# Two products of the keys on VectorE, denominators on TensorE, and two lists for the last part of an attention layer

## The chip, the cores and the metric

The kernel runs on one core of one Trainium2 chip. A core has five engines that run side by side, each through its own queue in order: TensorE (PE: matmuls and transposes), VectorE (DVE), ScalarE (ACT), GpSimd (POOL) and SyncE (SP, which issues most DMAs). Matrix products land in PSUM, everything else lies in SBUF. The metric is device time of one execution in microseconds; less is better. Comparisons use the median of several runs. One further execution was recorded by the profiler; all rows of the profile belong to that one.

## What is computed

Four graph layers follow each other on a graph of N = 2708 nodes with 128 features. Each is `x = x + layer(relu(layernorm(x)), adj)`. The change lies in layer 1, an attention with one head of 8 numbers for each of 128 channels d:

```python
q = (x @ Wq.T).reshape(d, n, h)        # d = 128, n = 2708, h = 8; k and v likewise
a = jnp.einsum('dnh,dmh->dnm', q, k) * scale
a = a + spatial_encoding + edge_encoding   # both are adj
a = jax.nn.softmax(a, axis=2)
out = jnp.einsum('dnm,dmh->dnh', a, v).reshape(n, h * d)
return out @ Wo.T
```

`adj` is nearly all zeros (some five entries a row). The kernel uses this. For all pairs of nodes without an edge the exponential of q·k is a polynomial of third degree in q and k, so the sums over m can be taken once as moments of the keys and evaluated for each query. For the pairs with an edge the kernel adds what the edge changes: exp(q·k) (exp(2 adj) - 1), times v for the numerator and alone for the denominator.

## The kernel before

**The pairs of channels.** The main loop of layer 1 runs over D = 64 pairs d of channels. Each pass has six chunks c. A chunk turns features of the queries (`turn`: transposes f_ps on PE, a copy fT on ACT), evaluates them against the weighted moments (`evaluate`: matmuls g_ps on PE, L1538; then on DVE the product z, L1546, and a reduction o_raw, L1555), and prepares what later passes need: the queries' features fq of pair d+1 (products on DVE through `mul_v`, L802), the moments m_ps of pair d+1 (PE, L869), and the keys' features fk of pair d+2 (products on POOL through `mul_g`, L805). `features` holds the products under names: "p0" to "p2", "xy" (16 products for each node, 704 numbers per partition), "t0" (10 products, 440 numbers), "t1", "t2". Which chunk makes which is written out in the tables `turns_q` and `turns_k`: "xy" in chunk 2, "t0" in chunk 3. For queries one operand is a copy in PSUM (kq_ps); for keys both are in SBUF (kv_t). `with_values` makes y, the keys' values times their first features (POOL, 704 numbers, twice a pass).

**The slots.** Between the chunks a generator `first` is advanced: 1.75 steps a chunk at the start, 4 from `faster` on, when `from_neighbours` begins. This walks over 121 slots b: a tile t of 128 nodes (sorted by number of neighbours) and one neighbour of each. A slot takes six steps: `load` fetches keys and values of the neighbours (indirect DMA, POOL's queue, L1235) for slot b+2, and `values` multiplies the values of slot b-2 by their weights (DVE, L1274); `store`, and `logits` of slot b (a product of 1024 numbers on POOL, L1250); `summed` reduces it for slot b-1 into c_c in PSUM (DVE, L1256); `added` adds slot b-2 to the tile's sum by a matmul with the identity (PE, L1291, v_ps); `weigh` (slot b-1: ACT, exponential and weight in place in c_c; in a tile's first slot also a copy c_den); `copied_out` at a tile's end. The denominators are added in `values` by DVE (c_den, L1282), in all slots of a tile but the first.

**The last part.** When the slots are over, each chunk takes up to four `step`s of other work: `normalise(u)` loads the two parts of a unit's sums (SP), adds them (POOL, L1395), takes reciprocals (DVE, L1400), multiplies (DVE, L1405) and stores the result in o_d (SP, L551); `projected(t)` loads 128 nodes from o_d (SP, L1034), transposes (PE, L1043), multiplies by Wo (PE, L1061) and adds to x (DVE, L1065). A unit is two groups of four channels, but for the last two units, which are one group each. All stand in one list, `beside`, taken strictly in order; a head of the list that cannot start holds up the rest. A generator yields how many chunks it wants to wait (LOAD is 4). What is left after the last pass is worked off in a loop of its own, and then layer 2 begins (L1846).

All instructions stand in the queues in the order of this code; the framework adds the waits.

Of the kernel before, what the change touches and what calls it, by code (L numbers as in the profile page):

```python
# [46 lines left out]
def gnn4_kernel(  # L47
# [687 lines left out]

    def features(mul, k, k2, f, most):

        T = k.shape[1]
        n = k.shape[0]
        gs = k[:, :, :HEAD].rearrange("p t (g e) -> p t g e", g=2)  # L740
        hs = k2[:, :, :HEAD].rearrange("p t (g e) -> p t g e", g=2)
        two = f[:, :, XX : XX + 20].rearrange("p t (g w) -> p t g w", g=2)
        yy = f[:, :, YY : YY + 10]

        def pair(e, o):
            w = 3 - e
            mul(
                two[..., o : o + w],
                gs[..., e : e + 1].to_broadcast([n, T, 2, w]),
                hs[..., e + 1 : 4],  # L750
            )

        def triple(o, left, right):
            w, v = left.shape[2], right.shape[2]
            if v == 1:
                mul(f[:, :, o : o + w], left, right.to_broadcast([n, T, w]))
            else:
                mul(
                    f[:, :, o : o + w * v].rearrange("p t (a b) -> p t a b", a=v),
                    left[:, :, None].to_broadcast([n, T, v, w]),  # L760
                    right[:, :, :, None].to_broadcast([n, T, v, w]),
                )
# [8 lines left out]
        return {  # L771
            "sq": lambda: nc.scalar.activation(two[..., 3:7], gs, AF.Square),  # L772
            "lin": lambda: nc.scalar.copy(f[:, :, LIN : LIN + 4], k[:, :, 4:8]),
            "p0": lambda: pair(0, 0),
            "p1": lambda: pair(1, 7),
            "p2": lambda: pair(2, 9),
            "xy": lambda: triple(XY, k2[:, :, 0:4], k[:, :, 4:8]),
            "t0": lambda: triple(YYY, yy, k[:, :, 4:5]),
            "t1": lambda: triple(YYY + 10, yy[:, :, 4:], k[:, :, 5:6]),
            "t2": lambda: triple(YYY + 16, yy[:, :, 5:7], k[:, :, 6:8]),  # L780
            "n": norms_of,
        }
# [32 lines left out]

    copied, turned_ = {}, {}

    def of_pair(d, at):
# [11 lines left out]
    def keys(d):  # L830
# [4 lines left out]
        fks[d] = fkp[d % 2]  # L835
        return features(mul_g, kv, kv, flat(fks[d]), most2[:, 1, 2 * d : 2 * d + 2])

# [232 lines left out]

    LOAD, SOON = 4, 1

    with ExitStack() as ph:
# [135 lines left out]
        def from_neighbours():  # L1211
# [46 lines left out]
            def weigh(b):  # L1258
# [5 lines left out]
                nc.scalar.activation(c, c, AF.Copy, scale=cw[:sz, t, s0 : s0 + 1])  # L1264
                if s0 == 0:
                    dens[t] = sm.tile([P, C], FP, name="c_den")
                    nc.scalar.copy(dens[t][:sz], c)

            def values(b):
# [10 lines left out]
                )  # L1280
                if s0:
                    nc.vector.tensor_tensor(dens[t][:sz], dens[t][:sz], c, ALU.add)  # L1282

            def added(b):
# [5 lines left out]
                for j in range(2):  # L1290
# [72 lines left out]
        def unit_of(g):  # L1363
            return g // 2 if g < NG - 2 else g - NG // 2 + 1

        NU = unit_of(NG - 1) + 1

        def normalise(u):

            last, two = u == NU - 1, u < NU - 2  # L1370
            nh = GRP * (1 + two)
            h0 = nh * u if two else (NG - NU + u) * GRP
            g = h0 // GRP
# [49 lines left out]
        beside = []  # L1423
        done = 0
        late, final = [], []
        for t, (r0, sz) in enumerate(rows):
            need = unit_of(min((((r0 + sz) * P - 1) // N) // GRP, NG - 1))
            while done <= need:
                beside.append((done, done, True))
                done += 1  # L1430
                while late and late[0][1] <= done - 2:
                    beside.append(late.pop(0))
            if need < NU - 1:
                late.append((t, need, False))
            else:
                final.append(t)
        beside += late
        groups = [(t, min(t + 4, final[0])) for t in range(0, final[0], 4)]
# [22 lines left out]
        def sum_bank():  # L1461
            return ps_c.tile([P, 2, S, C], FP, name="c_c")[:, 0, 0]

# [5 lines left out]

        def begin(summed):  # L1470

            if not beside:
                return None
            i, need, norm = beside[0]
            last = norm and i == NU - 1
            if need >= summed and not last:
                return None
            if not norm and any(e[2] <= need for e in under_way):
                return None
            takes = 1 if norm and i >= NU - 2 else 2  # L1480
            for ring in ("big",) if norm else ("c_v", "c_q"):
                if sum(e[4] for e in rings[ring]) + takes <= room[ring]:
                    beside.pop(0)
                    gen = normalise(i) if norm else projected(i, ring)
                    entry = [gen, None, need if norm else NU, True, takes]
                    rings[ring].append(entry)
                    under_way.append(entry)
                    return entry
            return None

        def step(n, summed):
# [3 lines left out]
            if entry is None:  # L1495
                entry = begin(summed)
# [117 lines left out]
        with tc.manual_schedule():  # L1614
# [7 lines left out]
            for d in range(D):  # L1622
                asked, keyed = {}, {}
                for c in range(NCH):
# [60 lines left out]
            for e in under_way:  # L1685
                e[1] = min(e[1], n)
            while beside or under_way:
                if to_turn:
# [498 lines left out]
```

## Time and profile before

| What | us |
|---|---|
| median of 3 runs (2151.46 to 2160.33) | 2151.55 |
| the profiled execution, its time | 2157.09 |
| its span (first to last instruction) | 2155.3 |
| PE busy, share of the span | 1692.6 (79%) |
| DVE busy | 1444.2 (67%) |
| ACT busy | 931.8 (43%) |
| POOL busy | 1321.0 (61%) |
| first reduction of a slot (L1256) starts | 754.2 |
| last one starts | 1464.4 |
| last z of the pairs (L1546) starts | 1714.9 |
| layer 2's first matmul (L1846) starts | 1765.2 |

A row of the profile names a line of the kernel, the engine and operation, output<-inputs with their sizes (partitions x elements), how often it ran, its busy time in us and the mean of one in ns, and how long the engine was idle just before and for whom. Busy shares are averages over stages with different limits: what matters is which engine is full in the stage that a change touches. Durations of matmuls are modelled by the profiler and overlap each other.

### The profile page before, as it was taken

How to read it: one execution, taken by the hardware profiler on the slowest of the kernel's cores; microseconds unless marked ns; L12 is line 12 of the kernel's file. 1: busy time of each engine (PE TensorE's matmuls, PEld its weight loads, DVE VectorE, ACT ScalarE, POOL GpSimd, SP SyncE). 2: the span in 40 equal slices, each digit the busy share in tenths (PEclk: the TensorE clock that was granted, in tenths of full speed). 3: DMA queues.
4: the chain of work that ended last, by engine and by line, in shares of the span. 5: the costliest groups of instructions: out<-in, count | busy, mean ns of one | idle time of the engine just before them, and what ended most of it. 6: DMA issues, size and time to landing. Idle time of an engine off the chain costs nothing. (4 is left out here: it accounts for less than half of the span.)

```text
span 2155.3 us, 30079 instructions
## 1 busy us (share of the span) xinstructions
PE 1692.6 (79%) x10634; PEld 1348.4 (63%) x10634; DVE 1444.2 (67%) x3232; ACT 931.8 (43%) x2049; POOL 1321.0 (61%) x1363
## 2 busy tenths in 40 slices
PE   4767989988889788988888888888889769943442
PEld 3656864488789666666666665667889745423431
DVE  6899846366677788888888888877788720134331
ACT  3947744376677444444444444444445210021010
POOL 1343332066566699999999999997667210057762
PEclk9978999999999999999999999988999979965555
DMA  4755319778799676667766766764767757433331
GB/s 158 298 164 191 134 57 363 294 246 249 240 300 318 177 245 239 225 238 255 252 231 240 237 244 245 250 237 143 228 202 223 242 152 276 155 138 104 94 100 38
DMA packets 256854, 453.68 MB, mean 210 GB/s; under 512 B 112267, under 2 KB 180110, under 8 KB 231483
## 3 DMA queue, kind: packets, MB, share of 16 engines
q1 hardware_dynamic: 225459, 282.79, 39.6%
q0 software_dynamic: 31232, 168.86, 23.0%
q8 instruction: 85, 1.39, 0.3%
q14 instruction: 78, 0.64, 0.1%
HBM read 336.99 MB, written 114.60 MB: 210 GB/s over the span
## 5 line engine op out<-in xcount | busy, mean ns | idle before, releaser
L1538 PE MATMUL g_ps<-mw,fT 128*124 128x124 f32 x2816 | 377.9, 277 | 10.8 <-DVE mw L883 6.2
L869 PE MATMUL m_ps<-y,fk 123*128 123x128 f32 (+1 forms) x2816 | 372.6, 278 | 0.2 <-POOL fk L805 0.2
L1538 PEld LDWEIGHTS g_ps<-mw,fT 128*124 128x124 f32 x2816 | 344.5, 192 | 12.0 <-DVE mw L883 7.1
L869 PEld LDWEIGHTS m_ps<-y,fk 123*128 123x128 f32 (+1 forms) x2816 | 345.6, 194 | 1.3 <-issue 1.0
L1528 ACT COPY fT<-f_ps 128x496 f32<-128x496 f32 (+1 forms) x384 | 208.6, 543 | 242.1 <-PE f_ps L1524 239.9
L1291 PE MATMUL v_ps<-c_v,ident 128*128 128x512 f32 (+1 forms) x484 | 254.3, 651 | 74.7 <-DVE c_v L1274 74.0
L805 POOL TENSOR_TENSOR fk<-kv_t 128x264 f32<-128x264 f32 (+3 forms) x256 | 188.5, 761 | 186.4 <-ACT kv_t L833 185.6
L1546 DVE TENSOR_TENSOR z<-g_ps,bq 124x360 f32<-124x360 f32 (+1 forms) x384 | 191.1, 498 | 163.3 <-PE g_ps L1538 151.0
L1524 PE MATMUL f_ps<-ident,fq 124*128 124x124 f32 x1408 | 222.9, 278 | 94.1 <-DVE fq L802 63.8
L1250 POOL TENSOR_TENSOR c_kv<-c_kv,c_q 128x1024 f32<-128x1024 f32 (+1 forms) x121 | 284.3, 2350 | 5.0 <-DMA c_kv<-kv_n,srt 3.4
L1524 PEld LDWEIGHTS f_ps<-ident,fq 124*128 124x128 f32 x1408 | 167.4, 145 | 188.5 <-issue 90.1
L805 POOL TENSOR_TENSOR y<-kv_t 128x704 f32<-128x704 f32 x128 | 191.0, 1492 | 67.6 <-PE m_ps L869 67.0
L1555 DVE TENSOR_REDUCE o_raw<-z 124x72 f32<-124x360 f32 (+1 forms) x384 | 190.7, 497 | 13.2
L1291 PEld LDWEIGHTS v_ps<-c_v,ident 128*128 128x128 f32 (+1 forms) x484 | 86.8, 200 | 151.7 <-DVE c_v L1274 69.2
L1256 DVE TENSOR_REDUCE c_c<-c_kv 128x128 f32<-128x1024 f32 (+1 forms) x121 | 148.0, 1223 | 50.2 <-POOL c_kv L1250 47.7
L1263 ACT ACTIVATE c_c<-c_c 128x128 f32<-128x128 f32 (+1 forms) x121 | 31.7, 262 | 330.6 <-DVE c_c L1256 312.9
L805 POOL TENSOR_TENSOR fk<-fk,kv_t 128x440 f32<-128x440 f32 (+2 forms) x192 | 154.9, 821 | 5.5 <-ACT fk L772 5.3
L1274 DVE TENSOR_TENSOR c_v<-c_kv,c_c 128x1024 f32<-128x1024 f32 (+1 forms) x121 | 146.6, 1211 | 0.0
L1235 POOL DMA_INDIRECT c_kv<-kv_n,srt x121 | 118.0, 975 | 22.3 <-issue 8.6
L1974 POOL DMA_INDIRECT g<-tab_d,l_nbr x99 | 103.5, 1045 | 30.2 <-issue 29.8
L957 PE MATMUL qkv_ps<-wT,hT 128*128 128x512 f32 (+1 forms) x264 | 116.9, 601 | 0.4 <-ACT hT L438 0.4
L170 POOL TENSOR_TENSOR n_hot<-n_hot,n_fl 128x640 f32<-128x640 f32 (+1 forms) x22 | 34.0, 1545 | 119.6 <-DVE n_hot L164 116.0
(315 smaller groups left out, 2989.0 us busy)
## 6 DMA issues: line engine op xcount, KB each, us to landing
a_nat<-in_adj_dram SPq DMA_DIRECT2D x34, 1354.0 KB
raw<-qkv_d SPq DMA_DIRECT2D x128, 275.0 KB
qkv_d<-qkv SPq DMA_DIRECT2D x21, 1600.0 KB
n_raw<-qkv_d SPq DMA_DIRECT2D x96, 275.0 KB
kv_n<-n_kv SPq DMA_DIRECT2D x16, 1408.0 KB
fk<-in_adj_dram SPq DMA_DIRECT2D x12, 1354.0 KB
o_g<-o_raw SPq DMA_DIRECT2D x31, 396.0 KB
fq<-in_adj_dram SPq DMA_DIRECT2D x9, 1354.0 KB
```

The source lines that it names most:

```text
L805: nc.gpsimd.tensor_tensor(o, x, y, ALU.mult)
L869: nc.tensor.matmul(pms[d][:, :P], fks[d][:sz, t].rearrange("p i f -> p (i f)"), wide[h][:sz, o : o + P], start=t == 0, stop=t == NT - 1,)
L1235: nc.gpsimd.indirect_dma_start(out=kvs[b][:sz, e].rearrange("p c e k -> p (c e k)"), out_offset=None, in_=kv_n.rearrange("n c k -> n (c k) ...
L1250: nc.gpsimd.tensor_tensor(k, k, qs[t][:sz], ALU.mult)
L1256: nc.vector.reduce_sum(cs[b][:sz], kvs[b][:sz, 0, :, 0], axis=AX.X)
L1274: nc.vector.tensor_tensor(z[:sz], kv[:sz, 0, :, 1].rearrange("p (j c) k -> p j c k", j=2), c.rearrange("p (j c) -> p j c", j=2)[:, :, :, None]
L1291: nc.tensor.matmul(accs[t][:sz, j], ident[:sz, :sz], z[:sz, j].rearrange("p c k -> p (c k)"), start=s0 == 0, stop=s0 == ROOM[t] - 1,)
L1524: nc.tensor.transpose(pt[:, m, :USED], fqs[d][:USED, t0 + m].rearrange("p i f -> p (i f)"), ident[:USED, :USED])
L1528: nc.scalar.copy(fts[d, c][:, :n, :USED], pt[:, :n, :USED])
L1538: nc.tensor.matmul(pg[:USED, m, :USED], ft[:, m, :USED], mws[d][:, :USED], start=True, stop=True,)
L1546: nc.vector.tensor_tensor(z[:USED, : 2 * n], pg[:USED, :n] .rearrange("p m (i w) -> p (m i) w", i=2)[:, :, : VW * B_ALL] .rearrange("p a ( ...
L1555: nc.vector.reduce_sum(ros[g][:USED, t0 : t0 + n, i : i + 2].rearrange("p m i k -> p m (i k)"), z[:USED, : 2 * n].rearrange("p (m i) k b - ...
```

## The change

During the slots (from `faster` to the end of `first`, while the list `crowded` holds something) the keys' products "xy" and "t0" are made by `mul_v` on DVE instead of `mul_g` on POOL. The denominators of the slots are no longer added on DVE: `weigh` copies the weights of every slot to c_den (ACT), and `added` adds that copy by one more matmul with the identity, into a third or fourth quarter of the PSUM tile c_c, which grows from [P, 2, S, C] to [P, 4, S, C] (S = 1, C = 128). `copied_out` reads it there.

In the last part the list `beside` becomes two, `to_norm` and `to_project`. A new unit is tried first; a projection starts when all units that it reads are `settled`, LAND = 4 chunks after their stores were issued. The last six groups are units of their own. LOAD becomes 5, and `normalise` ends with its store.

```diff
-    def features(mul, k, k2, f, most):
+    def features(mul, k, k2, f, most, heavy=None):
...
-        def triple(o, left, right):
+        def triple(o, left, right, mul=mul):
...
-            "xy": lambda: triple(XY, k2[:, :, 0:4], k[:, :, 4:8]),
-            "t0": lambda: triple(YYY, yy, k[:, :, 4:5]),
+            "xy": lambda: triple(XY, k2[:, :, 0:4], k[:, :, 4:8], heavy or mul),
+            "t0": lambda: triple(YYY, yy, k[:, :, 4:5], heavy or mul),
...
-        return features(mul_g, kv, kv, flat(fks[d]), most2[:, 1, 2 * d : 2 * d + 2])
+        return features(
+            mul_g, kv, kv, flat(fks[d]), most2[:, 1, 2 * d : 2 * d + 2],
+            mul_v if crowded else None,
+        )
...
-    LOAD, SOON = 4, 1
+    LOAD, SOON, LAND = 5, 1, 4
...
-            c_two = ps_c.tile([P, 2, S, C], FP, name="c_c")
+            c_two = ps_c.tile([P, 4, S, C], FP, name="c_c")
...
-                if s0 == 0:
-                    dens[t] = sm.tile([P, C], FP, name="c_den")
-                    nc.scalar.copy(dens[t][:sz], c)
+                dens[b] = sm.tile([P, C], FP, name="c_den", bufs=3)
+                nc.scalar.copy(dens[b][:sz], c)
...
-                if s0:
-                    nc.vector.tensor_tensor(dens[t][:sz], dens[t][:sz], c, ALU.add)
...
+                nc.tensor.matmul(
+                    c_two[:sz, 2 + t % 2, 0],
+                    ident[:sz, :sz],
+                    dens.pop(b)[:sz],
+                    start=s0 == 0,
+                    stop=s0 == ROOM[t] - 1,
+                )
...
-                    nc.scalar.copy(acc[:sz, :, HEAD], dens.pop(t)[:sz])
+                    nc.scalar.copy(acc[:sz, :, HEAD], c_two[:sz, 2 + t % 2, 0])
...
-            return g // 2 if g < NG - 2 else g - NG // 2 + 1
-
-        NU = unit_of(NG - 1) + 1
+            return g // 2 if g < 2 * TWOS else g - TWOS
+
+        TWOS = NG // 2 - 3
+        NU = NG - TWOS
...
             store_heads(nc.sync, h0, on)
-            yield SOON
...
+            crowded.append(True)
...
+        def begin(n, summed):
+
+            entry = None
+            if to_norm and (to_norm[0] < summed or to_norm[0] == NU - 1):
+                u = to_norm[0]
+                entry = enter("big", 1 + (u < TWOS), normalise(u), u)
+                if entry is not None:
+                    to_norm.pop(0)
+            if entry is None and to_project:
+                t, need = to_project[0]
+                if all(settled.get(u, n + 1) <= n for u in range(need + 1)):
+                    for ring in ("c_v", "c_q"):
+                        if entry is None:
+                            entry = enter(ring, 2, projected(t, ring), None)
+                    if entry is not None:
+                        to_project.pop(0)
+            return entry
...
+                if entry[2] is not None:
+                    settled[entry[2]] = n + LAND
...
+                            crowded.clear()
```

More of the change, by code (lines that the diff above doesn't have):

```diff
@@ L816, in gnn4_kernel @@
     copied, turned_ = {}, {}
+    crowded = []
     def of_pair(d, at):
@@ L1363, in unit_of @@
         def unit_of(g):
-            return g // 2 if g < NG - 2 else g - NG // 2 + 1
-        NU = unit_of(NG - 1) + 1
+            return g // 2 if g < 2 * TWOS else g - TWOS
+        TWOS = NG // 2 - 3
+        NU = NG - TWOS
         def normalise(u):
-            last, two = u == NU - 1, u < NU - 2
+            last, two = u == NU - 1, u < TWOS
             nh = GRP * (1 + two)
-            h0 = nh * u if two else (NG - NU + u) * GRP
+            h0 = nh * u if two else (TWOS + u) * GRP
             g = h0 // GRP
@@ L1419, in faster @@
             pace[0] = 4.0
+            crowded.append(True)
             yield
         first = chain(by_node(), sorted_rows(), faster(), from_neighbours())
-        beside = []
-        done = 0
-        late, final = [], []
+        to_norm, to_project = list(range(NU)), []
+        final = []
         for t, (r0, sz) in enumerate(rows):
             need = unit_of(min((((r0 + sz) * P - 1) // N) // GRP, NG - 1))
[L1428 to L1432, printed above, removed]
             if need < NU - 1:
-                late.append((t, need, False))
+                to_project.append((t, need))
             else:
                 final.append(t)
-        beside += late
+        settled = {}
         groups = [(t, min(t + 4, final[0])) for t in range(0, final[0], 4)]
@@ L1461, in sum_bank @@
         def sum_bank():
-            return ps_c.tile([P, 2, S, C], FP, name="c_c")[:, 0, 0]
+            return ps_c.tile([P, 4, S, C], FP, name="c_c")[:, 0, 0]
         def projected(t, ring):
@@ L1468, in projected, with enter @@
             yield from project_out(both, turn_bank, sum_bank, woT, t)
-        def begin(summed):
-            if not beside:
-                return None
[L1474 to L1489, printed above, removed]
+        def enter(ring, takes, gen, unit):
+            if sum(e[4] for e in rings[ring]) + takes > room[ring]:
+                return None
+            entry = [gen, None, unit, True, takes]
+            rings[ring].append(entry)
+            under_way.append(entry)
+            return entry
[14 more added lines that the diff above has]
+                        to_project.pop(0)
+            return entry
         def step(n, summed):
@@ L1495, in step @@
             if entry is None:
-                entry = begin(summed)
+                entry = begin(n, summed)
             if entry is None:
@@ L1686, in gnn4_kernel @@
                 e[1] = min(e[1], n)
-            while beside or under_way:
+            while to_norm or to_project or under_way:
                 if to_turn:
```

## The prediction

> **What bounds the kernel now.** I read the page's engine rows over 40 slices first, then the busy time of each engine in the stretches between landmarks, then waits and timelines inside them. The chain that ended last names only the final 3 us and is of no use here.
>
> ```profile
> DVE  6899846366677788888888888877788720134331
> POOL 1343332066566699999999999997667210057762
> 759.00:1469.40 710.40, 611.44 (x3782) 457.76 (x3782) 596.84 (x1090) 309.86 (x813) 677.71 (x552) 0.97 0.68 239
> 1469.40:1716.00 246.60, 214.35 (x1780) 206.23 (x1780) 196.97 (x432) 109.00 (x252) 148.69 (x114) 0.94 0.71 207
> 1716.00:1760.00 44.00, 23.71 (x112) 20.17 (x112) 13.07 (x32) 9.52 (x21) 7.26 (x3) 0.67 0.65 187
> ```
>
> The last three rows give, after the length, PE, weight load, DVE, ACT, POOL, clock, DMA share and GB/s. In the stretch of the slots POOL is busy 677.7 of 710.4 us (95%): it is the bound. The stretch holds 60 rows of L883, two for each pair of channels d, so it is 30 pairs of 23.68 us; per pair POOL has 22.59 us of work, PE 20.38, DVE 19.89, ACT 10.33. Afterwards PE is nearest its limit (214 of 247 us), and from 1716 to 1760 nothing is: a drain of loads, normalisation and out-projection that follow each other. The change touches all three.
>
> **Products moved to DVE.** Per form, in the slots:
>
> ```profile
> L805 POOL TENSOR_TENSOR fk<-kv_t 128x704 f32<-128x704 f32 x30 | 44.1, 1469 | 0.6
> L805 POOL TENSOR_TENSOR fk<-fk,kv_t 128x440 f32<-128x440 f32 x30 | 31.7, 1058 | 0.0
> L1282 DVE TENSOR_TENSOR c_den<-c_den,c_c 128x128 f32<-128x128 f32 x98 | 27.4, 280 | 0.0
> L802 DVE TENSOR_TENSOR fq<-bq,kq_ps 128x704 f32<-128x704 f32 x30 | 26.4, 878 | 0.0
> ```
>
> "xy" and "t0" take 1.47 + 1.06 = 2.53 us per pair from POOL: 22.59 becomes 20.06. DVE gets them at 0.88 us (the query's product of the same shape, fourth row) and 0.61 us (mean of the query's 440-element form), and loses the additions to c_den, 27.4/30 = 0.91 us. So DVE becomes 19.89 + 0.88 + 0.61 - 0.91 = 20.47 us. "t0" reads what POOL wrote a chunk earlier and "n" reads none of it, so no new wait on data arises.
>
> But the query's products have one operand in PSUM (kq_ps); the key's have both in SBUF (kv_t). The only DVE product in this trace with two SBUF operands beside a busy POOL is L1405:
>
> ```profile
> 1495.14 2.17 DVE L1405 TENSOR_TENSOR r_c<-r_o,r_rs 128x704 f32<-128x704 f32 x2
> 1495.19 4.23 POOL L805 TENSOR_TENSOR fk<-kv_t 128x264 f32<-128x264 f32 x4
> 1498.51 3.33 DVE L1405 TENSOR_TENSOR r_c<-r_o,r_rs 128x704 f32<-128x704 f32 x2
> 1499.38 1.70 POOL L805 TENSOR_TENSOR fk<-fk,kv_t 128x440 f32<-128x440 f32 x1
> ```
>
> Undisturbed it takes 0.88 us (its minimum), on average 1.34, at most 3.19; POOL's own 440-element product took 1.70 instead of 1.06 us beside it. The Trainium skill, "SBUF — State Buffer", section "SBUF: two separate sides", has the rule that speaks against the change: a DVE instruction with two SBUF inputs and a GpSimd instruction exclude each other for their whole length. By rows of busy time alone POOL gains 2.53 us per pair; by the rule it gives back the products' 1.49 and gains 1.04. The rows side with the rule. DVE's own wait for a POOL product under way: from 0 to 2.35 us each (POOL's longest product); at L1405's mean excess (1.34 - 0.88 = 0.46) two would be 0.9 us per pair. I take 0.4, because part falls where DVE waits anyway.
>
> **Denominators on TensorE.** One 128x128 matmul per slot, two passes. Nearest row: m_ps<-y,fk, 8 passes in 1.06 us of which 0.28 is one pass's own length, so 0.12 us per pass: 4 x 0.24 = 0.95 us per pair, PE 21.3 us. ACT's 99 further copies cost 0.265 us each (the 22 existing ones), 0.9 us per pair, hidden: ACT is busy 44%.
>
> What is not hidden is where the sum lies. c_two grows to [P, 4, 1, 128] floats, 2 KB a partition, and holds both the logits' sums (written by DVE, rewritten by ACT, read by DVE) and now the matmul's target. The Trainium skill, "PSUM — Partial Sum Buffer", section "PSUM bank collisions raise a hardware error", says that two engines may not touch one 2 KB bank at once, different columns and reads included, so that software has to order them. That this program is so ordered shows in before:
>
> ```profile
>   DVE tab L1951: 8.7, 7
> ACT fq L773 <- DVE fq L802: 10.7, 17, 0.7
> ```
>
> The first stands in the answer on the PSUM tile ab_ps, under who waited for its users: DVE did, 8.7 us, seven times of seven, although L1951 reads other columns of it than ACT's L1950. In the second ACT's copy from kq_ps waits for DVE's product from it, without using its result. So the dens matmul of slot b-2 will wait for DVE's reduction of slot b-1 emitted before it, and everything behind it on PE with it: transposes f_ps and products g_ps, for which DVE's next z waits. By columns alone this wait would be nothing; by bank it is what the order of the queues makes it. The phase of slots against chunks is fixed (6 steps against 4): in chunks 0 and 3 the reduction is a chunk ahead of its matmul, in chunks 2 and 5 directly ahead. Chunk 2:
>
> ```profile
> 1001.97 1.98 PE L1291 MATMUL v_ps<-c_v,ident 128*128 128x512 f32 x4 [0.31 <-DVE c_v L1274]
> 1002.84 0.88 DVE L802 TENSOR_TENSOR fq<-bq,kq_ps 128x704 f32<-128x704 f32 x1
> 1003.64 1.22 DVE L1256 TENSOR_REDUCE c_c<-c_kv 128x128 f32<-128x1024 f32 x1
> 1003.79 0.59 PE L1524 MATMUL f_ps<-ident,fq 124*128 124x124 f32 x4
> 1005.28 0.53 DVE L1546 TENSOR_TENSOR z<-g_ps,bq 124x360 f32<-124x360 f32 x1 [0.42 <-PE g_ps L1538]
> ```
>
> PE runs ahead: f_ps starts at 1003.79 while DVE reduces until 1004.86, and z then waits only 0.42 us. Afterwards f_ps must follow the matmul, which follows the reduction; the key's "xy" stands just ahead of that reduction too. From the reduction's end to z: hand-over 0.06, matmul 0.24, then f_ps to z as above, 1005.28 - 1003.79 = 1.49: 1.8 us in which DVE is idle. In chunk 5 likewise. Two per pair make 3.6 us, against 0.42 + 0.77 at the same places of the pair at 1000 us.
>
> **Sum of a pair.** Before, DVE: 19.89 busy + 1.96 waiting for g_ps (58.8 us in all idle before z) + 1.4 for POOL's logits (42.3 us) + small ones = 23.68. After: 20.47 busy + 3.6 at the two places + 0.5 left of the other waits before z (0.77 before) + 0.4 for the port + 0 for POOL (2.5 us lighter) = 24.97. That is +1.29 us, over 30 pairs +39 us. PE's own account agrees: 21.3 work + about 2 stalled + 1.5 still waiting for c_v = 24.8. So the bound moves from POOL to the loop DVE-PE-DVE, and POOL's gain is idle time. Bounds: -1.0 us (no bank wait) to +1.7 (port wait at 0.9), -30 to +51 us.
>
> **The last part.** Six last groups become units of their own (two before), normalisation goes ahead of projection, and a projection's load is issued four chunks after the store that it needs. From 1480 to 1716 SP stood some 47 us for PE at L1034 and 89 for DVE at L551, but hardly anybody in the loop waited for that: PE's wait for o_nat is 0.6 us there. What can shrink is the drain:
>
> ```profile
> 1711.38 11.57 SPq L1034 DMA_DIRECT2D o_nat<-o_d  x1
> 1725.29 3.54 POOL L1395 TENSOR_TENSOR r_o<-r_o,r_c 128x1584 f32<-128x1584 f32 x1 [21.93 <-DMA r_c<-more_n]
> 1744.31 1.86 POOL L1395 TENSOR_TENSOR r_both<-o_raw,r_both 128x792 f32<-128x792 f32 x1 [12.50 <-DMA r_both<-more_n]
> ```
>
> A double unit is still added at 1725, ten us after the last z, and the last unit at 1744 only, because its load stood behind o_nat loads. Four projections (transposes from 1720 on) lie in the drain. Afterwards, from the last z at 1716: addition of the unit of group 30 1.9, reciprocal and product 1.6, store and load of o_nat about 7 (as from the store at 1733.4 to the transposes at 1741.9, less what stood between), transposes and copies 3, sums 3.7, addition and statistics 0.9, normalising and turning the last group about 6 (1753 to 1760): 24 us instead of 44. Against -20: three projections move into the PE-bound loop at 1.04 + 1.95 = 3.0 us, +9. The finer units cost four more of each: five issues on SP at 0.3 to 0.6 us, which stand beside waits; a reciprocal pair 2 x 0.68 instead of 1.25, nothing. Together -11 us, bounds -25 and +8 (PE pays, drain stays).
>
> **Forecast.** The profiled execution has a span of 2155.3 and a time of 2157.09 us; the median of the three runs is 2151.55, 5.5 less, and I count from it: 2151.55 + 39 - 11 = 2179.5; a profiled execution would show about 2185.
>
> **Rivals.**
> 1. *POOL was the bound and is relieved* (faster). If PE's wait at the bank is absent or covered, a pair is POOL's 20.06 + 1.09 gaps + 1.49 lost to the port = 22.6, -32 us; with -11: 2108. It decides once the two stalls cost DVE under 0.3 us each beyond today's. For it: POOL's 95%. Against it: the seven waits of ab_ps. 12%.
> 2. *The stall is half covered*: PE has slack of 3 us per pair and DVE can run values ahead; a pair then stays near 23.9, +7, with -11: 2148, no difference that can be told. 16%.
> 3. *The last part pays too*: slots at the upper bound +51, last part +8: 2211. For it: PE at 87% there. 12%.
>
> The forecast itself, 2160 to 2200 as its own range, gets 60%. A measurement of this kernel tells about 0.5% (10.8 us) from no change. Rival 1 and a sliver of 2 are faster: 0.14; most of 2 and the forecast's lowest edge no change: 0.15; the rest slower: 0.71. The range 2142 to 2206 leaves out rival 1 and most of 3.
>
> **What would show it.** Right: POOL in the slots falls to about 85%; PE's matmul into c_c waits for DVE's L1256 some 2 us per pair; idle time before z rises from 59 to over 100 us; the stretch of the slots grows to about 750 us; the key's products on DVE show means above 0.88 and 0.61 with maxima over 2 us; the drain from last z to L2's first matmul shrinks by some 20 us. Wrong: POOL still over 92% with a shorter stretch (rival 1), or a longer stretch with no wait of PE at c_c, which would leave the port alone to blame.

## The result, and the profile after

The changed kernel takes 2302.13 us (median of 4 runs, 2298.21 to 2308.45) against 2154.41 us for the kernel before in the same comparison: a ratio of 1.0685, 95% interval 1.0648 to 1.0721. It is slower, as forecast, but by 148 us, where 28 were forecast and 2206 us was the upper end of the range.

The profiled execution of the changed kernel took 2298.21 us (span 2296.4), 141.1 us more than that of before. The table splits this at the same landmarks in both traces: first row of L883 (L887 after) in the slots, the same row behind the last slot, last z, layer 2's first matmul.

| stage | before | after | change | forecast |
|---|---|---|---|---|
| slots, 30 pairs | 710.4 | 830.6 | +120.2 | +39 |
| loop, to the last z | 245.5 | 268.3 | +22.8 | +9 |
| drain, to layer 2 | 50.3 | 51.1 | +0.8 | -20 |
| the rest | 1149.1 | 1146.4 | -2.7 | 0 |

The engine rows over 40 slices of the changed kernel's page:

```profile
DVE  6899754566778777777777777776878840042332
POOL 1334222266656777767777677774666500027774
```

In the slots (slices 14 to 28) POOL's row shows sixes and sevens where it stood at nines before. Neither row has a nine there, and by the busy times below no other engine is near its limit, so no engine is the bound by its work alone. These are the busy times in the three stages (stretch, length, then PE, weight load, DVE, ACT and POOL busy, clock, DMA share, GB/s):

```profile
758.86:1589.42 830.56, 668.99 (x4021) 508.44 (x4020) 646.12 (x1052) 329.75 (x912) 614.18 (x492) 0.95 0.58 204
1589.42:1857.70 268.28, 212.31 (x1690) 204.31 (x1690) 204.37 (x425) 104.33 (x241) 155.81 (x116) 0.87 0.72 203
1857.70:1908.80 51.10, 29.83 (x206) 25.65 (x206) 14.03 (x43) 15.53 (x34) 2.15 (x7) 0.84 0.31 107
```

In the slots POOL is at 614 of 831 us (74%), PE at 81%, DVE at 78%. DVE stands idle for 184 us of it. For whom, the list of waits in the slots says (who waited <- for whom: us in all, times, longest):

```profile
ACT c_c L1267 <- PE c_c L1299: 441.9, 119, 8.9
DVE z L1556 <- PE g_ps L1548: 137.5, 60, 3.4
PE c_c L1299 <- DVE c_c L1260: 83.5, 51, 5.5
...
DVE c_v L1277 <- ACT n_kv L1320: 18.4, 17, 1.7
...
DVE c_v L1277 <- ACT c_den L1270: 12.7, 26, 0.5
```

Before, the wait of z in the slots was:

```profile
DVE z L1546 <- PE g_ps L1538: 51.2, 46, 3.3
```

L1299 is the new matmul for the denominators. PSUM holds more than matrix products here: DVE writes the logits' sums into c_c, and ACT works on them there. The matmul waits 83.5 us for DVE's reduction L1260, which writes other columns of the same PSUM bank and whose result it does not read; ACT's exponential of those logits in turn is released by the matmul. DVE's z, two stations behind it on PE, waits 137.5 us instead of 51.2. The last two rows of the first list are new altogether: DVE's values now wait for ACT's copies out of the same bank.

One chunk of the timeline shows the chain (start, length, engine, line, and in brackets the idle time before it):

```profile
1018.72 1.98 PE L1292 MATMUL v_ps<-c_v,ident 128*128 128x512 f32 x4 [0.53 <-DVE c_v L1277]
...
1019.40 0.88 DVE L802 TENSOR_TENSOR fq<-bq,kq_ps 128x704 f32<-128x704 f32 x1
...
1020.20 0.89 DVE L802 TENSOR_TENSOR fk<-kv_t 128x704 f32<-128x704 f32 x1
...
1021.00 1.22 DVE L1260 TENSOR_REDUCE c_c<-c_kv 128x128 f32<-128x1024 f32 x1
...
1022.36 0.46 PE L1299 MATMUL c_c<-c_den,ident 128*128 128x128 f32 x2 [1.66 <-DVE c_c L1260]
...
1022.66 0.59 PE L1534 MATMUL f_ps<-ident,fq 124*128 124x124 f32 x4
...
1024.15 0.53 DVE L1556 TENSOR_TENSOR z<-g_ps,bq 124x360 f32<-124x360 f32 x1 [1.94 <-PE g_ps L1548]
```

Compare with the same chunk before: there f_ps started while DVE was still reducing. Here PE idles 1.66 us until the reduction ends at 1022.22, and then DVE idles 1.94 us until PE has come round to g_ps. The two engines take turns. The key's product "xy" (1020.20) stands between the query's product and the reduction, so PE waits for it too.

Finally the key's products themselves, in groups by shape, in the slots:

```profile
L802 DVE TENSOR_TENSOR fk<-kv_t 128x704 f32<-128x704 f32 x30 | 51.2, 1706 | 0.0
...
L802 DVE TENSOR_TENSOR fk<-fk,kv_t 128x440 f32<-128x440 f32 x30 | 18.2, 606 | 0.0
```

"xy" has a mean of 1.71 us where it takes 0.89 by itself (median 0.887, longest 4.72); "t0" has 0.61, its undisturbed length.

The 30 pairs are not alike. In 18 of them "xy" met no wait (0.885 to 0.889 us) and the pair took 26.3 us on average; in the other 12 it took 1.12 to 4.72 us and the pair 29.7. The granted clock of TensorE differs too: of the 18 pairs without that wait, 11 had a clock of 1.00 (0.995 or more) and took 25.9 us, seven had 0.94 and took 27.0. One pair of each kind, columns as above:

```profile
1033.45:1059.03 25.58, 21.23 (x134) 16.06 (x134) 20.67 (x37) 10.26 (x29) 22.22 (x18) 1.00 0.59 208
1451.28:1478.62 27.34, 22.71 (x134) 17.09 (x134) 20.76 (x37) 11.34 (x31) 21.02 (x18) 0.94 0.70 251
1280.33:1312.60 32.27, 23.64 (x134) 18.59 (x134) 24.68 (x37) 11.22 (x31) 21.30 (x18) 0.89 0.62 215
```

### The profile page after: what moved, and what is told of

Its sections match the earlier page's. It is cut to its first block, busy times and chain, and to the rows that moved or that the text cites. A ratio compares the mean times of both kernels' runs of the same rounds, so it can differ in the third digit from the quotient of the medians.

```text
span 2296.4 us, 30731 instructions
## 1 busy us (share of the span) xinstructions
PE 1757.6 (77%) x10876; PEld 1403.8 (61%) x10876; DVE 1504.1 (65%) x3196; ACT 952.9 (41%) x2149; POOL 1259.8 (55%) x1303
## 5 line engine op out<-in xcount | busy, mean ns | idle before, releaser
L1548 PE MATMUL g_ps<-mw,fT 128*124 128x124 f32 x2816 | 393.9, 284 | 9.3 <-DVE mw L887 7.5
L873 PE MATMUL m_ps<-y,fk 123*128 123x128 f32 (+1 forms) x2816 | 380.2, 282 | 0.0
L1548 PEld LDWEIGHTS g_ps<-mw,fT 128*124 128x124 f32 x2816 | 361.2, 200 | 10.3 <-DVE mw L887 8.3
L873 PEld LDWEIGHTS m_ps<-y,fk 123*128 123x128 f32 (+1 forms) x2816 | 354.3, 198 | 1.0 <-issue 1.0
L1534 PE MATMUL f_ps<-ident,fq 124*128 124x124 f32 x1408 | 232.3, 286 | 100.0 <-DVE fq L802 62.7
L1292 PE MATMUL v_ps<-c_v,ident 128*128 128x512 f32 (+1 forms) x484 | 247.7, 636 | 67.0 <-DVE c_v L1277 64.8
L805 POOL TENSOR_TENSOR fk<-kv_t 128x264 f32<-128x264 f32 (+3 forms) x225 | 145.1, 671 | 209.8 <-ACT kv_t L834 209.3
L1260 DVE TENSOR_REDUCE c_c<-c_kv 128x128 f32<-128x1024 f32 (+1 forms) x121 | 148.0, 1223 | 8.3 <-POOL c_kv L1254 2.9
L1299 PEld LDWEIGHTS c_c<-c_den,ident 128*128 128x128 f32 (+1 forms) x242 | 44.1, 203 | 165.7 <-issue 155.2
L805 POOL TENSOR_TENSOR fk<-fk,kv_t 128x440 f32<-128x440 f32 (+2 forms) x161 | 124.6, 791 | 14.7 <-ACT fk L772 14.5
L1299 PE MATMUL c_c<-c_den,ident 128*128 128x128 f32 (+1 forms) x242 | 54.9, 311 | 83.5 <-DVE c_c L1260 83.5
```

Of the source, the lines that this page charges most:

```text
L805: nc.gpsimd.tensor_tensor(o, x, y, ALU.mult)
L873: nc.tensor.matmul(pms[d][:, :P], fks[d][:sz, t].rearrange("p i f -> p (i f)"), wide[h][:sz, o : o + P], start=t == 0, stop=t == NT - 1,)
L1260: nc.vector.reduce_sum(cs[b][:sz], kvs[b][:sz, 0, :, 0], axis=AX.X)
L1292: nc.tensor.matmul(accs[t][:sz, j], ident[:sz, :sz], z[:sz, j].rearrange("p c k -> p (c k)"), start=s0 == 0, stop=s0 == ROOM[t] - 1,)
L1534: nc.tensor.transpose(pt[:, m, :USED], fqs[d][:USED, t0 + m].rearrange("p i f -> p (i f)"), ident[:USED, :USED])
L1548: nc.tensor.matmul(pg[:USED, m, :USED], ft[:, m, :USED], mws[d][:, :USED], start=True, stop=True,)
```

## The experiments

All times are medians, with the ratio to the kernel before from runs on the same chip. "Slots", "loop" and "drain" are the stages of the table above, from each one's own trace. Traces of kernels whose code for a stage is the same differ by 0.7 us in the slots (710.3 to 711.0, before and the three runs with lists alone), but in the loop by 10 us (245.0 to 254.7) and in the drain by 6 (48.3 to 53.8), so smaller differences there say nothing.

### The parts one at a time

**Products only.** The first two edits of the change: `heavy`, `crowded`, and nothing else.

```diff
+            "xy": lambda: triple(XY, k2[:, :, 0:4], k[:, :, 4:8], heavy or mul),
+            "t0": lambda: triple(YYY, yy, k[:, :, 4:5], heavy or mul),
```

> Before, with the keys' xy and t0 on VectorE during the slots and nothing else. Bank theory (the denominators' matmul in the bank of c_c ties TensorE to VectorE, and that is where the time went): this part alone is harmless, POOL loses 2.53 us per pair and gets back at most 1.5 of it at the port, so the slots take 680 to 715 us (710 before) and the kernel 2120 to 2160. Port theory (products with two SBUF operands stop POOL and are stopped by it): slots of 760 us and more, kernel above 2200.

Measured: 2183.97 us, ratio 1.0117 (1.0095 to 1.0139); slots 735.1, that is +24.7. By itself the edit already loses: more than the bank theory expected and less than the port theory. In groups by shape in its slots:

```profile
L802 DVE TENSOR_TENSOR fk<-kv_t 128x704 f32<-128x704 f32 x30 | 62.8, 2093 | 0.0
L802 DVE TENSOR_TENSOR fk<-fk,kv_t 128x440 f32<-128x440 f32 x30 | 34.1, 1136 | 0.0
```

2.09 and 1.14 us, 1.21 and 0.53 more than undisturbed: 1.7 us per pair. DVE is busy 686 of 735 us (93%), POOL 623 (85%): the bound has gone from POOL to DVE. What one such product waits for is seen in the timeline at 1085 us:

```profile
1084.77 2.36 POOL L1254 TENSOR_TENSOR c_kv<-c_kv,c_q 128x1024 f32<-128x1024 f32 x1
1085.65 3.67 DVE L802 TENSOR_TENSOR fk<-kv_t 128x704 f32<-128x704 f32 x1
1087.08 1.48 POOL L805 TENSOR_TENSOR y<-kv_t 128x704 f32<-128x704 f32 x1
1088.71 1.46 POOL L1239 DMA_INDIRECT c_kv<-kv_n,srt  x1 [0.15 <-POOL y L805]
```

DVE's product begins 0.88 us into a product of POOL's. It ends at 1089.32, which is 0.76 us after the end of POOL's *second* product at 1088.56, about its own length (0.88). So it stood through two of them, as far as start and end can tell.

**Denominators only.** The matmul, the copies and the wider c_c; products stay on POOL.

```diff
-                if s0:
-                    nc.vector.tensor_tensor(dens[t][:sz], dens[t][:sz], c, ALU.add)
...
+                nc.tensor.matmul(
+                    c_two[:sz, 2 + t % 2, 0],
...
```

> Before, with the denominators as matmuls into c_c and the products left on POOL. Bank theory: TensorE waits for the reduction and VectorE's z for TensorE, as in the whole change: slots of 770 to 820 us, kernel 2215 to 2265, waits before z above 110 us. Port theory: POOL remains the bound, slots of 705 to 720 us, kernel 2150 to 2165.

Measured: 2198.70 us, ratio 1.0174 (1.0153 to 1.0196); slots 749.5 (+39.1), less than the 770 to 820 expected. Its waits in the slots:

```profile
DVE z L1550 <- PE g_ps L1542: 117.9, 59, 2.9
...
PE c_c L1295 <- DVE c_c L1256: 37.5, 54, 0.9
DVE c_v L1273 <- ACT n_kv L1316: 20.1, 17, 1.8
DVE c_v L1273 <- ACT c_den L1266: 8.9, 17, 0.5
```

The wait at the bank, the longer wait before z and the wait for ACT are all there without the products. DVE was given 0.91 us less work per pair and the pair became 1.30 us longer.

**Both, without the lists.**

> The whole change without the lists of the last part. If the slots alone made the 120 us that their stretch grew by, and the 20 us after them come from the lists: 2260 to 2285. If the 20 us behind the slots are carried over from the slots: 2295 to 2310.

Measured: 2279.79 us, ratio 1.0562 (1.0539 to 1.0585); slots 830.3, loop 246.9, drain 48.4. This has the slots of the changed kernel and the last part of the one before. So the lists have no part in the slots' loss, and the two other edits together cost 119.9 us there, 56 more than their 24.7 and 39.1 one by one.

**The lists alone.**

> Before, with the two lists, the finer units and LAND, and neither of the other two parts. If the lists cost what the last part lost in the whole change (projections pushed into the drain): 2170 to 2180, with 7 or 8 projections after the last z. If they bring what the prediction said: 2135 to 2150, with one or two.

Measured: 2181.83 us, ratio 1.0095 (1.0079 to 1.0112); slots 711.0, loop 264.6 (+19.1), drain 53.4 (+3.1). The last part loses by itself, and the drain that was to shrink has not. Counting the transposes L1043 by eights, seven projections lie in the drain, against four before.

### Is it the port?

"The port" is the forecast's word for the access to SBUF for which, by the rule that it names, a VectorE product with two SBUF operands and a GpSimd instruction exclude each other.

**Products with one operand in PSUM.** The key's products on DVE take their second operand from kq_ps instead of kv_t: same instruction, same size. The kernel leaves out the key's own factor there.

```diff
+            "xy": lambda: triple(XY, k2[:, :, 0:4], (kq if heavy else k)[:, :, 4:8], heavy or mul),
+            "t0": lambda: triple(YYY, yy, (kq if heavy else k)[:, :, 4:5], heavy or mul),
```

> As the products-only kernel, but the second operand of xy and t0 on VectorE is the query's copy in PSUM (kq_ps) in place of the key's in SBUF: same shapes, other numbers, so the attention's values are not the reference's. Port theory: the means fall from 2.09 and 1.14 us to 0.88 and 0.61, POOL and VectorE stop excluding each other, and the slots take 660 to 695 us (735 with two SBUF operands, 710 before); kernel 2110 to 2140. If VectorE's added work as such was the cost: slots of 720 to 740 us.

Measured: 2133.48 us, ratio 0.9873 (0.9852 to 0.9894); slots 690.3. Its groups by shape:

```profile
L802 DVE TENSOR_TENSOR fk<-kv_t,kq_ps 128x704 f32<-128x704 f32 x30 | 26.4, 882 | 0.0
L802 DVE TENSOR_TENSOR fk<-fk,kq_ps 128x440 f32<-128x440 f32 x30 | 18.1, 604 | 0.0
```

The same products in the same places take 0.88 and 0.60 us. The slots are 44.9 us shorter than with both operands in SBUF and 20.1 shorter than before. So the loss of the products came from both operands lying in SBUF; without it, the relief of POOL is worth 20 us.

### Is it the bank?

**The new matmul into v_ps's bank.** The same matmul, copies and dropped additions, but the target is a bank that PE writes just before anyway. The kernel leaves out all of a denominator but its last slot, which ACT copies from SBUF.

```diff
+                nc.tensor.matmul(
+                    accs[t][:sz, 1, :C],
+                    ident[:sz, :sz],
+                    dens[b][:sz],
+                    start=False,
...
```

> As the denominators-only kernel, with the same copies on ScalarE and the same matmul per slot, but into the bank of the values' sums (v_ps), which no other engine touches within a tile; c_c stays a tile for VectorE and ScalarE alone. The weights are so added to values of 16 channels, and the denominator is the last slot's weight only. Bank theory: the waits of TensorE for c_c's reduction and the longer waits before z are gone, slots 700 to 715 us (749 with c_c's bank), kernel 2150 to 2165. If TensorE's two more passes per slot cost the time: 745 us and more.

Measured: 2160.71 us, ratio 1.0011 (0.9998 to 1.0023); slots 710.3, as before. Its waits in the slots:

```profile
ACT c_c L1264 <- DVE c_c L1257: 294.0, 108, 4.2
...
DVE c_c L1257 <- POOL c_kv L1251: 57.0, 44, 2.8
DVE z L1552 <- PE g_ps L1544: 45.8, 42, 2.9
```

ACT's exponential is released by DVE again, z waits 46 us for g_ps where it was 51 before (64 in all where it was 59), the values wait for nobody, and DVE waits for POOL's logits: POOL is the bound once more. The matmul's work (PE busy 623 instead of 611 us) is hidden. All of the 39 us came from where the matmul writes (and ACT reads its sum at a tile's end). The target moved to another bank and to another tile at once, so no run tells whether the waits that the framework adds go by the one or the other.

**Both cured.** The products with an operand in PSUM and the matmul in v_ps's bank; what those two kernels leave out is left out here.

> Products and denominators moved, both with their cure (operand from kq_ps; matmul into v_ps), the last part as before; the attention's numbers are as wrong as in those two. If port and bank hold the whole loss of the slots, also the 57 us that the two parts cost together beyond the sum of each alone: slots of 640 to 690 us, kernel 2090 to 2140. If a third coupling (ScalarE's copies, the ring of buffers) is in it: above 730 us.

Measured: 2126.34 us, ratio 0.9833 (0.9809 to 0.9857); slots 671.1, 39 us shorter than before, at the same work and engines for which the changed kernel took 830.6. So the change's aim was sound; the 160 us between lie in two places where operands live. In 29 of its 30 pairs the granted clock is 1.00.

### What is wrong with the lists?

In the run of the lists alone the loop lost 19 us though it holds fewer projections. Its DVE timeline, reciprocals and products of the units:

```profile
1497.64 1.26 DVE L1401 RECIPROCAL r_rs<-r_o 128x176 f32<-128x176 f32 x1 [0.26 <-POOL r_o L1396]
1498.93 4.99 DVE L1406 TENSOR_TENSOR r_c<-r_o,r_rs 128x704 f32<-128x704 f32 x2
1503.85 1.24 DVE L1401 RECIPROCAL r_rs<-r_o 128x176 f32<-128x176 f32 x1
1505.13 3.26 DVE L1406 TENSOR_TENSOR r_c<-r_o,r_rs 128x704 f32<-128x704 f32 x2
```

Two units were started in one chunk and arrive at DVE together: 10.8 us without a gap in which neither fq nor z can pass. The loop has three such double groups (10.7, 10.0 and 8.3 us); before it had one (8.0). The products have two operands in SBUF, so they wait for POOL as well (mean 1.64 us instead of 1.32). PE's waits in that loop:

```profile
PE f_ps L1525 <- DVE fq L802: 38.3, 10, 10.4
```

Before:

```profile
PE f_ps L1524 <- DVE fq L802: 15.7, 9, 6.9
```

The granted clock is lower as well, 0.89 instead of 0.94, but that is not the main loss: PE is busy for 208 us of the loop (214 before) and stands idle for 57 (31 before). Two experiments try the bursts.

**One unit at a time.** A unit may start only when none is under way.

```diff
-            if to_norm and (to_norm[0] < summed or to_norm[0] == NU - 1):
+            if to_norm and not any(e[2] is not None for e in under_way) and (to_norm[0] < summed or to_norm[0] == NU - 1):
```

> As the lists-only kernel, but a unit is started only when no other unit is under way. Burst theory (two units in one chunk put reciprocals and multiplications of some 9 us in front of VectorE's products of the pairs, for which TensorE waits): the loop after the slots falls from 265 to 245-252 us (245 before). If projections pushed to the end are what costs: the loop stays near 265, or the drain grows by what the loop loses, kernel 2175 to 2190.

Measured: 2223.93 us, ratio 1.0294 (1.0276 to 1.0312); loop 229.5, drain 133.8. The loop is even shorter than expected and PE's wait at f_ps falls to 18.0 us, 4.4 at most. But units fell so far behind that nine projections and the last units were left to the drain. It shows the burst's cost only roughly: the loop held 11 projections instead of 16, and at the forecast's 3.0 us each that alone makes 245.5 - 15 = 230.5. On the same count the loop of the lists alone, with 13 transposed and 12 multiplied, should have been about 235; it took 264.6. So an estimate of the bursts' cost is 30 us.

**Projections first.** If it were the order of precedence, trying a projection before a unit should mend it.

> As the lists-only kernel, with a projection tried before a new unit. If it is the precedence of units that leaves projections for the drain: at most four after the last z, loop of 245 to 265 us, drain of 40 to 48, kernel 2145 to 2165. If finer units and LAND cost by themselves: kernel as lists-only, 2175 to 2190.

Measured: 2184.68 us, ratio 1.0113 (1.0074 to 1.0151); loop 279.6, drain 46.5. Precedence is not the cause: the loop became longer still, and it has three double groups as well.

### A version that keeps what was sound

The PSUM tile of kq_ps has free columns. ACT copies the two key columns that the products need there (one copy per pair), so that DVE's products read one operand from PSUM and compute what they should. There is room for two of four columns: half of "xy", all of "t0", and "t1" if wanted. The denominators stay on DVE.

```diff
+            nc.scalar.copy(ps, kv[:, :, 4:6])
...
+            def halves():
+                triple(XY, k2[:, :, 0:4], ps, mul_v)
+                triple(XY + 8, k2[:, :, 0:4], k[:, :, 6:8])
...
+            made["t0"] = lambda: triple(YYY, yy, ps[:, :, 0:1], mul_v)
+            made["t1"] = lambda: triple(YYY + 10, yy[:, :, 4:], ps[:, :, 1:2], mul_v)
```

Without the last line it is the first of these runs, with it the second.

> Before, with t0 and half of xy moved to VectorE during the slots through PSUM operands that are right: ScalarE copies the key's fifth and sixth feature (88 numbers) into free columns of kq_ps. POOL loses 1.06 + 0.73 us per pair, VectorE gains 0.61 + 0.45, ScalarE 0.3. If port and bank are all there is: slots of 685 to 700 us, kernel 2128 to 2145, against 2159 for before. If the copy into the bank of kq_ps makes VectorE and ScalarE wait for each other: slots above 705 us.

Measured: 2155.91 us, ratio 0.9988 (0.9968 to 1.0008), over a spread of 2143.8 to 2173.67; slots 711.9, where 685 to 700 were expected. No gain. Its PE was busy 643 us in the slots where the second had 615, at a lower clock; why is open.

> As best_a, with t1 on VectorE too (operand also from the copied columns): POOL loses another 0.77 us per pair, VectorE gains 0.45. As POOL is then at 20 and VectorE at 21.4 us per pair, as with both whole products from PSUM: slots of 680 to 695 us, kernel 2122 to 2140; no better than best_a by more than 8 us, since VectorE is then as near its limit as POOL.

Measured: 2145.71 us, ratio 0.9941 (0.9924 to 0.9958); slots 695.2, loop 247.5, drain 48.8. Faster than before by 0.6%, less than expected, with DVE's three key products at 0.52, 0.60 and 0.45 us.

**With lists that don't burst.** The same, and the lists of the change, but a unit starts only four chunks after the one before it.

```diff
+            if to_norm and (
+                to_norm[0] == NU - 1 or (to_norm[0] < summed and n >= begun_at[0] + 4)
+            ):
...
+                    begun_at[0] = n
```

> The products of best_b (operand copied to PSUM, t0, half of xy and t1 on VectorE, no denominator matmul) with the lists for the last part, but a unit is begun only four chunks or more after the one before it. All parts of the computation are there. Slots as in best_b, 690 to 700 us. If the lists' loss is the burst of two units begun in one chunk: loop 235 to 248 us, drain 46 to 55, kernel 2135 to 2150 us. If the finer units cost by themselves, wherever they stand: loop 260 us or more, kernel 2160 to 2175 us.

Measured: 2131.50 us, ratio 0.9860 (0.9839 to 0.9882); slots 699.6, loop 237.1, drain 46.5. It is the fastest that computes everything: 1.4% below the kernel before. Its units on DVE stand apart now:

```profile
1485.98 1.25 DVE L1417 RECIPROCAL r_rs<-r_o 128x176 f32<-128x176 f32 x1
1487.27 2.56 DVE L1422 TENSOR_TENSOR r_c<-r_o,r_rs 128x704 f32<-128x704 f32 x2
1498.25 1.24 DVE L1417 RECIPROCAL r_rs<-r_o 128x176 f32<-128x176 f32 x1
1499.53 3.20 DVE L1422 TENSOR_TENSOR r_c<-r_o,r_rs 128x704 f32<-128x704 f32 x2
```

and PE's wait for fq in the loop is the shortest of all:

```profile
PE f_ps L1545 <- DVE fq L811: 11.7, 11, 3.3
```

The finer units and the wait of four chunks behind a store are as in the changed kernel; only the bursts are gone, and the loop is 27.5 us shorter than with the lists alone. With projections first, loop and drain hold as many projections as here (14 transposed and 13 multiplied in the loop) and the drain is as long, but the loop is 42 us longer. The loop's gain over before, 8.4 us, is within the scatter of this stage; two transposes and three multiplications fewer would make 8 (an estimate from the forecast's 1.04 and 1.95 us).

## Why the prediction was right in direction and wrong in size

**The mechanism of the slots held.** "The dens matmul of slot b-2 will wait for DVE's reduction of slot b-1 emitted before it, and everything behind it on PE with it" is what the waits and the timeline of the changed kernel show, and the run with the matmul in another bank shows that the place makes it. What the forecast took from the Trainium skill, "PSUM — Partial Sum Buffer", section "PSUM bank collisions raise a hardware error", agrees with these traces: the program keeps even unlike columns of one bank in order, and two readers as well (values behind L1320). They show the order, not what would come of a collision, and bank and tile are the same here. Where the forecast expected no wait by columns, the edit alone cost 39 us. Its two signs for this in the trace of before were weaker than it took them for: L1950 and L1951 also write one SBUF tile (tab), L773 and L802 another (fq), and that could order them too. The rival in which POOL's relief decides fell with it: POOL went to 74%, but nobody was waiting for it.

**The step that failed is the sum of a pair**, "20.47 busy + 3.6 at the two places + 0.5 left of the other waits before z + 0.4 for the port + 0 for POOL = 24.97". Its terms as the traces have them, in us per pair:

| DVE | forecast | after | denominators only | products only |
|---|---|---|---|---|
| busy, port wait included | 20.87 | 21.54 | 19.37 | 22.87 |
| waiting before z | 4.1 | 4.58 | 4.03 | 1.13 |
| values waiting for ACT | 0 | 1.04 | 1.02 | 0 |
| other gaps | 0 | 0.53 | 0.56 | 0.50 |
| a pair | 24.97 | 27.69 | 24.98 | 24.50 |

That the denominators alone come to the 24.98 forecast for both is a coincidence: they lack the products' work and have waits that the forecast left out.

- *The port, taken at 0.4.* It is 0.82 in the changed kernel (1.71 - 0.89 for "xy", nothing for "t0") and 1.7 for the products alone. The reason given for taking less than the excess of L1405, "part falls where DVE waits anyway", fails in the changed kernel: against the denominators alone, the wait before z did not shrink with the products but grew from 4.03 to 4.58. It holds in part for the products alone, where that wait fell from 1.96 to 1.13. The bound "from 0 to 2.35 us each (POOL's longest product)" is wrong too, since two POOL products can pass in succession: the longest "xy" was 4.72, 3.83 above its own length. The rule of the Trainium skill, "SBUF — State Buffer", section "SBUF: two separate sides", by which a VectorE instruction with two SBUF inputs and a GpSimd instruction that reads SBUF exclude each other for their whole length, agrees: 1.71 us with both operands in SBUF (2.09 for the products alone), 0.88 with one in PSUM.
- *The values' wait for ACT, 1.04, was not in the sum at all.* It is the same bank again: ACT's copy out of the denominators' quarter (L1320) reads it, and DVE's values, which read another quarter, come behind it. The copies into c_den (L1270) add to it because ACT's exponential is held up by the matmul: with the matmul in v_ps's bank the same copies are there and no value waits. The forecast followed the bank's order for PE and called ACT's copies "hidden: ACT is busy 44%". Busy share says nothing of who waits for a copy.
- *Other gaps, 0.53,* were in the sum of before ("small ones", 0.43) and were dropped in that of after.
- *The waits before z* were sized well: 4.58 for 4.1. The remaining 0.25 of busy time is overlap that was lost: DVE's rows by shape sum to 58 us more than its busy time before, and to 51 after.

The differences make 2.7 us per pair, 81 us over 30: the whole gap between +39 and +120. The granted clock has no row of its own in this sum. By the pairs without a wait of "xy" (25.9 us at 1.00, 27.0 at 0.94) it is worth about 0.6 us per pair here, an estimate: 1.1 us in 17 of 30 pairs. Whether the stalls lower the clock or the clock draws out the stalls stays open.

**Why the two edits cost more together.** Before, DVE had 3.8 us of idle time per pair. Alone, the products mostly fill it (busy 22.87, idle 1.6), and alone, the matmul at the bank turns it into waits that stand on the way. Together, each us that the products add to DVE is paid in full: from the denominators alone to both, busy time grows by 2.17 and the wait before z by 0.55, and the pair by 2.71. PE's wait at the bank grows from 37.5 us (0.9 at most) to 83.5 (5.5 at most), since "xy" stands ahead of the reduction for which the matmul waits. The longest of each belong together:

```profile
1294.48 4.72 DVE L802 TENSOR_TENSOR fk<-kv_t 128x704 f32<-128x704 f32 x1
...
1300.49 0.76 PE L1299 MATMUL c_c<-c_den,ident 128*128 128x128 f32 x2 [5.50 <-DVE c_c L1260]
```

This is read from the accounts; a run with the bank cured and the port not, or the reverse, would tell it apart and was not made. The forecast's check, "PE's own account agrees", could not catch this: PE waits for DVE and DVE for PE, so either account closes at whatever length the loop has.

**The last part, forecast at -11, came at +22 to +24.** Of its two terms, "24 us instead of 44" for the drain fell: the drain's own works were followed as if the queue were empty, but seven projections stood there, not one. Fewer projections got into the loop (13 transposed and 12 multiplied instead of 16), not three more; what part of that is the wait of four chunks behind a store was not tried. And "+9 for three projections in the loop" had the wrong cause of a loss: the loop lost 23 us with fewer projections in it, mainly by units that start together and hold DVE for up to 10.8 us. "The finer units cost four more of each … nothing" holds: with the starts spread they cost nothing that can be seen.

**What was to show it.** Right: PE's wait at L1260 (2.8 us per pair for "some 2"), the idle time before z (137.5 for "over 100"), "xy" with its maximum. Wrong: the stretch of 750 us, "t0" above 0.61, POOL at 85% and the drain. The third rival's bounds for the slots (+51) and the last part (+8) were both too near: the bounds took each term's own upper end and left out the waits that had no term. By its own terms the upper bound is +1.79 us a pair and +54 (1.29 + 0.9 - 0.4), which changes nothing.

## What to carry to other kernels

Before an operation is given to another engine, ask where its operands and its target live, not only how long it takes: two SBUF operands on VectorE beside a full GpSimd cost about twice their time here with the products alone, one in PSUM nothing, and a matmul into a bank that two other engines work in cost 39 us where another bank cost none. When two engines wait for each other within a chunk, work on either is no longer hidden by idle time of the other; sum the loop, with every wait on every engine that touches the shared bank, and don't lower a wait because the engine "waits anyway". Work that is started by precedence alone comes in bursts: spacing the starts was worth more than its order.

## What the runs showed of the hardware

- A VectorE product that had to wait for GpSimd let two GpSimd products in succession pass (1085 us in the run of the products alone, 1294 us in the changed kernel) and ended while GpSimd was issuing a DMA; the wait reached 3.8 us, more than any single GpSimd product lasts (2.38 at most).
- In the changed kernel "t0" met no such wait in any of 30 cases (597 to 612 ns), with GpSimd at 74%, while in the run of the products alone it took 1.14 us on average, with GpSimd at 85%. The wait goes by what stands opposite in the chunk: when "t0" began, GpSimd ran no product in any of the 30 cases of the changed kernel, and it ran one in 26 of 30 with the products alone. "xy" in the changed kernel began beside a product 12 times, of which 11 had a wait, and beside the issue of a DMA 18 times, of which one had (the 4.72 us, where a product followed at once).
- In the loop the granted clock was 0.94 before and with spread starts, 0.89 with the lists alone and 0.87 after, although PE's busy time hardly differed (214, 211, 208 and 212 us). With the loop's code unchanged it lay between 0.91 and 0.94, and the longest of these loops (254.7 us) had the lowest.
